# The last routed second products put between chunks of the first ones, and a fourth inner layer transposed by PE

## The chip, the cores and the metric

The kernel runs on one core of a Trainium2 chip. The metric is device time in microseconds (us) of one execution. Five executions of the kernel before took 523.51 to 530.28 us, with a median of 528.0 us. One further execution was profiled; its own time stands beside its span in the table below.

## The reference

The input x has 4 batches of 512 rows of width 512 (2,048 rows in all). A cross-attention is added first, then a feed-forward layer with one shared expert and eight routed ones, of which each row uses two:

```
x = x + tanh(g_xattn) * attention(layernorm(x), ctx)
z = layernorm(x)
swiglu(z, Wg, Wu, Wd) = (silu(z @ Wg) * (z @ Wu)) @ Wd      # D = 512, H = 352
top_v, top_i = top_k(sigmoid(z @ Wr + br + rb), 2); top_v normalised to sum 1
x = x + tanh(g_ffn) * (swiglu(z, shared) + sum over e of w[:, e] * swiglu(z, expert e))
```

All numbers are float32.

## The kernel before, in words

**Up to the routed experts** the kernel makes the attention of the four batches, the first product of the shared expert, the routing (which writes a list of rows for each expert), and the second product of the shared expert, whose result it writes to the output in device memory. The weights of all eight routed experts then stay in one buffer (`wbig`).

**The routed experts** take the list in blocks of 128 rows that belong to one expert. There are at most `NBLK` = 39 blocks; `SURE` = 37 of them are always made, numbers 0 to 36 (`last` = 36), and two more only if the routing needs them (`spare_blocks`, under a condition that was false here). The whole loop is written out when the program is built. A block i has these steps:

- `gather(i)`, L752: four indirect DMAs, issued from POOL, fetch the block's rows into one of four buffers. The gather of block i+3 is made to wait for the silu of block i.
- `block_turned(i)`, L822: DVE turns the rows (a stream transpose of 128x512, L326) into one of two buffers `xgT_v[i % 2]`. It can't be written before the first product of block i-2 has read it.
- `block_hidden(i)`, L779: the **first product**. `part(cs)` makes, for each chunk c of `ND` = 4, one matmul into `rg` and one into `ru` (L790, each of them two passes on PE in the profile). `finish()` then makes silu on ACT (L798) and the multiplication on DVE, into the inner layer `hr_v[i % 2]` (L800, or in two pieces at L810 for the blocks that PE transposes).
- The inner layer must be transposed before the second product can use it. For blocks below `SURE - NEAR` it goes through device memory: `hidden_moved(i)`, L825, issues two SP DMAs (L764 writes, L767 reads back into one of three buffers `zhr_v`), and DVE turns what came back (128x384, L326) into `hTr_v[i % 2]`. For the last `NEAR` = 3 blocks, 34, 35 and 36, `hidden_transposed_near(i)`, L837, has PE transpose it in three pieces (L840) and DVE copy the result out of PSUM (L841).
- `block_second(k)`, L843: the **second product** of three matmuls (L570, six passes in the profile), then ACT scales the result by the rows' weights (L817, into one of three buffers `y_v`) and POOL issues one indirect DMA (L818) that adds the 128 rows to the output in device memory. Each of these adds waits for the one before it, because all of them write the same output.

**The order.** Iteration i of the loop makes the first product of block i and then the second product of block i-2; that is the lag. Behind the loop stands block 36 with what is then left over:

```
    part, finish = block_hidden(last)
    hidden_transposed_near(last - 2)
    block_second(last - 2)
    part([0])
    hidden_transposed_near(last - 1)
    block_second(last - 1)
    part(range(1, ND))
    finish()
```

and after that the transposes and the second product of block 36 itself. Within an engine the instructions run in a fixed order. That order is not the order of the lines: when the program is built, a planner takes for each engine the earliest written instruction that its own model holds for ready. So the trace can have an instruction ahead of one that is written before it.

Of the kernel before, what the change touches and what calls it, by code (L numbers as in the profile page):

```python
# [22 lines left out]
def flamingo_block(  # L23
# [25 lines left out]
    NS, ND, NCC, NN = S // P, D // P, C // P, N // P  # L49
# [79 lines left out]
    zhr_v = [sp.take(NQ, HQ) for _ in range(3)]  # L129
    hTr_v = [sp.take(NF, P) for _ in range(2)]  # L130
    assert sp.at <= (B - 1) * NS * D

    def after(later, earlier, reason="written before it is read"):
        tc.add_manual_dep(
            later.ins, earlier.ins.name,
            mybir.DependencyInfo(mybir.DependencyClass.Sync, mybir.DependencyReason.DATA),
            reason=reason,
        )
# [185 lines left out]
    def turn(z, dst):  # L324

        return nc.vector.transpose(  # L326
            dst.rearrange("p c (j b) -> p b c j", b=NQ), z.rearrange("p b (c i) -> p b c i", i=Q)
        )
# [237 lines left out]
    def down(hT, wdj):  # L566

        po = ps_out.tile([P, D], F32, tag="out", name="po")
        for j in range(NF):
            product["last"] = nc.tensor.matmul(  # L570
                po, lhsT=hT[:, j, :], rhs=wdj(j), start=(j == 0), stop=(j == NF - 1)
            )
        return po
# [27 lines left out]
    def shared_out(b, lo=0, hi=NS, behind=None):  # L601
        for n in range(b * NS + lo, b * NS + hi):
            if n == 0:
                shared_turned(0, behind[0])
                shared_turned(1, behind[1])
            elif n + 1 < B * NS:
                shared_turned(n + 1)
            shared_back(n + AHEAD, product.get("out"))
            done = product["out"] = shared_down(n)
        return done  # L610
# [141 lines left out]
    def gather(i, behind=None, z=None):  # L752
        z = zx_v[i % 4] if z is None else z
        for q in range(NQ):
            g = nc.gpsimd.indirect_dma_start(  # L755
                out=z[:, q, :], out_offset=None,
                in_=xz_d, in_offset=at(idx4[:, q, i : i + 1]),
            )
            if behind is not None:
                after(g, behind, "not too many at once")  # L760
# [11 lines left out]
        nc.gpsimd.memset(h[:, H:], 0.0)  # L772

    n_used = nc.values_load(total_i[0:1, 0:1], min_val=0, max_val=NBLK)
    NEAR = 3
    SURE = NBLK - 2
    base = {}

    def block_hidden(i, xgT=None):  # L779
        xgT = xgT_v[i % 2] if xgT is None else xgT  # L780
        base[i] = nc.tensor.value_load(
            eoff_i[0:1, i : i + 1], min_val=0, max_val=(E - 1) * EW
        )
        pg = ps_mm.tile([P, H], F32, tag="mm", name="rg")
        pu = ps_mm.tile([P, H], F32, tag="mm", name="ru")

        def part(cs):
            for c in cs:
                for dst, lo in ((pg, 0), (pu, H)):
                    nc.tensor.matmul(  # L790
                        dst, lhsT=xgT[:, c, :],
                        rhs=wbig[:, bass.ds(base[i] + (c * 2 * H + lo), H)],
                        start=(c == 0), stop=(c == ND - 1),
                    )

        def finish():
            sg, h = sgr_v[i % 2], hr_v[i % 2]
            silu = nc.scalar.activation(sg, pg, AF.Silu)  # L798
            if i < SURE - NEAR:
                nc.vector.tensor_mul(h[:, :H], sg, pu)  # L800
                return silu

            full = H // HQ
            to = h.rearrange("p (c a i) -> p a c i", a=NQ, i=Q)
            for a, n, w in ((0, full, HQ), (full, 1, H - full * HQ)):
                x2, y2 = (
                    v[:, a * HQ : a * HQ + n * w].rearrange("p (a c i) -> p a c i", a=n, i=Q)
                    for v in (sg, pu)
                )
                nc.vector.tensor_mul(to[:, a : a + n, : w // Q, :], x2, y2)  # L810
            return silu

        return part, finish

    def block_out(i, po):
        y = y_v[i % 3]
        nc.scalar.activation(y, po, AF.Copy, scale=wts[:, i : i + 1])  # L817
        nc.gpsimd.indirect_dma_start(  # L818
            out=out, in_=y, out_offset=at(idx[:, i : i + 1]), in_offset=None, compute_op=ALU.add
        )  # L820

    def block_turned(i):  # L822
        return turn(zx_v[i % 4], xgT_v[i % 2])

    def hidden_moved(i):  # L825
        regroup(
            hr_v[i % 2], zhr_v[i % 3],
            dram.tile([NQ * P, HQ], F32, tag=f"by{HQ}", name="by", bufs=4),
        )
# [3 lines left out]
    turned = block_turned(0)  # L833
# [3 lines left out]
    def hidden_transposed_near(i):  # L837
        pt = ps_tr.tile([P, NF, P], F32, tag="tr", name="pt")
        for c in range(NF):
            nc.tensor.transpose(pt[:, c, :], hr_v[i % 2][:, ts(c, P)], ident)  # L840
        nc.vector.tensor_copy(hTr_v[i % 2], pt)  # L841

    def block_second(k):  # L843
        po = down(
            hTr_v[k % 2], lambda j: wbig[:, bass.ds(base[k] + (GU + j * D), D)]
        )
        block_out(k, po)

    def spare_blocks():

        sp = Space(wsd.rearrange("p c d -> p (c d)"), 0)
        zs = [sp.take(NQ, D // NQ) for _ in range(SURE, NBLK)]
        xgT = sp.take(ND, P)
        with tc.If(n_used > SURE):
            for i in range(SURE, NBLK):
                gather(i, z=zs[i - SURE])
            for i in range(SURE, NBLK):
                turn(zs[i - SURE], xgT)
                part, finish = block_hidden(i, xgT)
                part(range(ND))  # L860
                finish()
                hidden_transposed_near(i)
                block_second(i)


    last = SURE - 1
    for i in range(last):
        part, finish = block_hidden(i)
        part(range(ND))
        if i >= 2:  # L870
            turn(zhr_v[(i - 2) % 3], hTr_v[i % 2])
        nxt = block_turned(i + 1)
        if i == 0:
            after(nxt, turned, "its rows come later")
        silu = finish()
        if i < SURE - NEAR:
            hidden_moved(i)
        if i >= 2:
            block_second(i - 2)
        else:  # L880
            shared_out(B - 1, NS - 2 + i, NS - 1 + i)
        if i + 3 < SURE:
            gather(i + 3, silu)
        if i == last // 2:
            spare_blocks()

    part, finish = block_hidden(last)
    hidden_transposed_near(last - 2)
    block_second(last - 2)
    part([0])  # L890
    hidden_transposed_near(last - 1)
    block_second(last - 1)
    part(range(1, ND))
    finish()
    hidden_transposed_near(last)
    block_second(last)

# [53 lines left out]
```

## Time and profile before

| what | us |
|---|---|
| median of five executions | 528.0 |
| the profiled execution, its own time | 531.76 |
| its span, from the first to the last instruction | 529.8 |
| PE busy | 501.0 (95%) |
| POOL busy | 264.7 (50%) |
| DVE busy | 229.3 (43%) |
| ACT busy | 93.8 (18%) |
| PE busy from 260 to 480 us, of 220.00 | 219.18 |
| PE busy from 510 to 520 us, of 10.00 | 6.45 |

Starts are in us from the start of the span. "Matmul x2" in a row of the timeline is one float32 matmul of two passes. PE is the matmul engine, PEld its weight loads, SPq the DMA queue of SP. A bracket at the end of a row gives the engine's idle time before the instruction and what ended it.

### The profile page before, as it was taken

What the parts mean: (1) busy time and instruction counts of PE and PEld (TensorE: products, weight loads), DVE (VectorE), ACT (ScalarE), POOL (GpSimd) and SP (SyncE); (2) the same over time, 40 slices, a digit from 0 to 9 for tenths busy, and PEclk for the clock granted to TensorE, in tenths of its full rate; (3) what the DMA queues carried; (4) which work ended last, traced back from release to release, by engine and by line L of the source; (5) the groups of instructions that cost most, each with busy time, mean ns of one, the idle gap of its engine ahead of it and who ended that gap; (6) DMA issues with size and microseconds to landing.
All of it is one profiled execution on the core that took longest, in us unless ns stands there. A gap on an engine that the chain in (4) does not pass through costs nothing. (4 is left out here: it accounts for less than half of the span.)

```text
span 529.8 us, 5475 instructions
## 1 busy us (share of the span) xinstructions
PE 501.0 (95%) x1523; PEld 279.0 (53%) x1523; DVE 229.3 (43%) x542; ACT 93.8 (18%) x167; POOL 264.7 (50%) x290
## 2 busy tenths in 40 slices
PE   8999999998899959999999999999999999999981
PEld 4444564563577624445555555555555555555540
DVE  1898867842954206663423332233323332323210
ACT  3354035001042000000111111111111111111110
POOL 3005222170172620506677777777667777777231
PEclk9999999999799979999999999999999999999997
DMA  6999994398639998643466666666646566676333
GB/s 214 394 334 367 354 322 127 122 220 111 227 96 199 197 143 264 195 158 110 119 133 123 127 120 127 137 119 132 117 110 129 111 129 135 134 139 120 60 41 40
DMA packets 66590, 86.82 MB, mean 164 GB/s; under 512 B 32929, under 2 KB 39969, under 8 KB 66561
## 3 DMA queue, kind: packets, MB, share of 16 engines
q1 hardware_dynamic: 42480, 54.03, 35.0%
q0 software_dynamic: 13184, 25.88, 26.5%
q10 hardware_dynamic: 10896, 6.56, 5.2%
q8 instruction: 15, 0.25, 0.2%
q14 instruction: 15, 0.11, 0.1%
HBM read 55.73 MB, written 30.70 MB: 163 GB/s over the span
## 5 line engine op out<-in xcount | busy, mean ns | idle before, releaser
L755 POOL DMA_INDIRECT x_all<-xz_d,idx x148 | 141.3, 955 | 86.1 <-issue 35.7
L326 DVE STREAM_TRANSPOSE x_all<-x_all 128x512 f32<-128x512 f32 (+1 forms) x71 | 70.0, 986 | 159.5 <-DMA x_all<-by 131.1
L790 PE MATMUL rg<-wbig,x_all 128*128 x296 | 111.9, 460 | 1.7 <-issue 0.9
L790 PE MATMUL ru<-wbig,x_all 128*128 x296 | 111.7, 459 | 0.0
L570 PE MATMUL po<-wbig,x_all 128*128 x222 | 101.4, 592 | 0.7 <-DVE x_all L841 0.7
L790 PEld LDWEIGHTS rg<-wbig,x_all 128*128 128x128 f32 x296 | 55.9, 190 | 43.1 <-issue 18.4
L818 POOL DMA_INDIRECT out_x<-ws,idx x37 | 59.6, 1611 | 31.5 <-issue 17.5
L790 PEld LDWEIGHTS ru<-wbig,x_all 128*128 128x128 f32 x296 | 56.2, 190 | 31.3
L570 PEld LDWEIGHTS po<-wbig,x_all 128*128 128x128 f32 x222 | 42.1, 190 | 44.0 <-issue 36.3
L393 PE MATMUL po<-wbig 128*128 128x512 f32 x128 | 59.6, 618 | 3.4 <-DVE x_all L397 3.4
L466 PE MATMUL pg<-ws,wbig 128*128 128x352 f32 x128 | 50.6, 477 | 0.0
L466 PE MATMUL pu<-ws,wbig 128*128 128x360 f32 (+1 forms) x128 | 50.0, 473 | 0.0
L312 POOL TENSOR_TENSOR rstd<-ve,mhalf 128x4 f32<-128x4 f32 x8 | 8.2, 1022 | 79.3 <-DVE ve L310 39.2
L798 ACT ACTIVATE h_all<-rg 128x352 f32<-128x352 f32 x37 | 17.1, 463 | 171.9 <-PE rg L790 171.9
L570 PE MATMUL po<-wsd,wqk 128*128 128x512 f32 x96 | 42.3, 595 | 2.1 <-DVE eoff_i L700 2.1
L817 ACT ACTIVATE ws<-po,wts 128x512 f32<-128x512 f32 x37 | 25.4, 687 | 104.0 <-PE po L570 101.2
L393 PEld LDWEIGHTS po<-wbig 128*128 128x128 f32 x128 | 25.2, 199 | 34.8 <-issue 29.2
L554 POOL DMA_INDIRECT slot_d<-ent,posi x32 | 31.0, 967 | 24.2 <-DVE ent L543 10.5
L466 PEld LDWEIGHTS pu<-ws,wbig 128*128 128x128 f32 x128 | 24.9, 195 | 14.1 <-issue 1.0
L570 PEld LDWEIGHTS po<-wsd,wqk 128*128 128x128 f32 x96 | 18.0, 190 | 24.1 <-issue 20.3
L466 PEld LDWEIGHTS pg<-ws,wbig 128*128 128x128 f32 x128 | 23.8, 195 | 11.9 <-issue 1.0
L800 DVE TENSOR_TENSOR x_all<-h_all,ru 128x352 f32<-128x352 f32 x34 | 17.5, 516 | 12.5 <-PE ru L790 6.7
(133 smaller groups left out, 339.0 us busy)
## 6 DMA issues: line engine op xcount, KB each, us to landing
wbig<-in_Wgu SPq DMA_DIRECT2D x8, 1408.0 KB, 15.5
by<-x_all SPq DMA_DIRECT2D x34, 192.0 KB, 3.4
x_all<-by SPq DMA_DIRECT2D x34, 192.0 KB, 2.4
wbig<-in_Wd SPq DMA_DIRECT2D x8, 768.0 KB, 17.6
x_all<-in_x SPq DMA_DIRECT2D x4, 1024.0 KB, 11.9
wbig<-in_xT SPq DMA_DIRECT2D x4, 1024.0 KB, 10.0
xz_d<-wbig POOLq DMA_DIRECT2D x16, 256.0 KB, 4.7
out_x<-x_all SPq DMA_DIRECT2D x16, 256.0 KB, 3.0
```

The source lines that it names most:

```text
L312: power = nc.gpsimd.tensor_tensor(rstd, ve, mhalf, ALU.pow)
L326: return nc.vector.transpose(dst.rearrange("p c (j b) -> p b c j", b=NQ), z.rearrange("p b (c i) -> p b c i", i=Q))
L393: product["last"] = nc.tensor.matmul(po, lhsT=xT_v[b % 2][:, c, ts(s, P)], rhs=attT_v[b % 2][:, c, :], start=(c == 0), stop=(c == NN - 1),)
L466: product["last"] = nc.tensor.matmul(dst, lhsT=xnT_v[b % 2][:, c, ts(s, P)], rhs=ws[:, c, at : at + n], start=(c == 0), stop=(c == ND - 1),)
L554: sc = nc.gpsimd.indirect_dma_start(out=slot_d, in_=what, out_offset=bass.IndirectOffsetOnAxis(ap=where, axis=0), in_offset=None,)
L570: product["last"] = nc.tensor.matmul(po, lhsT=hT[:, j, :], rhs=wdj(j), start=(j == 0), stop=(j == NF - 1))
L755: g = nc.gpsimd.indirect_dma_start(out=z[:, q, :], out_offset=None, in_=xz_d, in_offset=at(idx4[:, q, i : i + 1]),)
L790: nc.tensor.matmul(dst, lhsT=xgT[:, c, :], rhs=wbig[:, bass.ds(base[i] + (c * 2 * H + lo), H)], start=(c == 0), stop=(c == ND - 1),)
L798: silu = nc.scalar.activation(sg, pg, AF.Silu)
L800: nc.vector.tensor_mul(h[:, :H], sg, pu)
L817: nc.scalar.activation(y, po, AF.Copy, scale=wts[:, i : i + 1])
L818: nc.gpsimd.indirect_dma_start(out=out, in_=y, out_offset=at(idx[:, i : i + 1]), in_offset=None, compute_op=ALU.add)
```

## The change

Four blocks instead of three have their inner layer transposed by PE: block 33 joins 34, 35 and 36 (`NEAR` = 4). The block behind the loop becomes a part of the loop. In the last four iterations the second products are written between the chunks of a first product, by a table whose keys are the iteration and the chunk ahead of which the product goes (`ND` = behind `finish()`) and whose values are the block: 31 ahead of chunk 3 of block 33; 32 ahead of chunk 2 of block 34; 33 ahead of chunk 1 of block 35 and 34 behind block 35; 35 ahead of chunk 3 of block 36. Block 36's own transposes and second product stay last.

```diff
-    NEAR = 3
+    NEAR = 4
...
     last = SURE - 1
-    for i in range(last):
+    seconds = {
+        (last - 3, 3): last - 5, (last - 2, 2): last - 4, (last - 1, 1): last - 3,
+        (last - 1, ND): last - 2, (last, ND - 1): last - 1,
+    }
+    for i in range(SURE):
         part, finish = block_hidden(i)
-        part(range(ND))
-        if i >= 2:
-            turn(zhr_v[(i - 2) % 3], hTr_v[i % 2])
-        nxt = block_turned(i + 1)
-        if i == 0:
-            after(nxt, turned, "its rows come later")
+        near = i > last - NEAR
+
+        def behind(c):
+            k = seconds[i, c]
+            if k < SURE - NEAR:
+                turn(zhr_v[k % 3], hTr_v[k % 2])
+            else:
+                hidden_transposed_near(k)
+            block_second(k)
+
+        if not near:
+            part(range(ND))
+            if i >= 2:
+                turn(zhr_v[(i - 2) % 3], hTr_v[i % 2])
+        else:
+            for c in range(ND):
+                part([c])
+                if (i, c + 1) in seconds and c + 1 < ND:
+                    behind(c + 1)
+        if i < last:
+            nxt = block_turned(i + 1)
+            if i == 0:
+                after(nxt, turned, "its rows come later")
         silu = finish()
         if i < SURE - NEAR:
             hidden_moved(i)
-        if i >= 2:
+        if near:
+            if (i, ND) in seconds:
+                behind(ND)
+        elif i >= 2:
             block_second(i - 2)
...
-    part, finish = block_hidden(last)
-    hidden_transposed_near(last - 2)
-    block_second(last - 2)
-    part([0])
-    hidden_transposed_near(last - 1)
-    block_second(last - 1)
-    part(range(1, ND))
-    finish()
     hidden_transposed_near(last)
     block_second(last)
```

## The prediction

> **What bounds the kernel now.** I first looked at the busy shares: PE is busy for 501.0 of 529.8 us, DVE for 43%, so I asked where PE waits in the stretch of the routed blocks, with the list of PE's waits from 260 us to the end and the busy times of two windows.
>
> ```profile
> PE 501.0 (95%) x1523; PEld 279.0 (53%) x1523; DVE 229.3 (43%) x542; ACT 93.8 (18%) x167; POOL 264.7 (50%) x290
> ...
> PE pt L840 <- DVE x_all L810: 0.8, 1, 0.8
> PE rg L790 <- ACTq L854: 0.8, 1, 0.8
> PE po L570 <- DVE x_all L841: 0.7, 1, 0.7
> ...
> 260.00:480.00 220.00, 219.18 (x660) 125.14 (x659) 69.88 (x91) 34.51 (x60) 162.96 (x151) 1.00 0.63 126
> 510.00:520.00 10.00, 6.45 (x19) 2.89 (x17) 1.14 (x3) 1.84 (x3) 2.18 (x2) 1.00 0.42 52
> ```
>
> The reader sees that from 260 us on PE waits three times, 0.8 us each; two of these lie in block 36: its transposes wait for the multiplication of its inner layer (L810), and its second product for the copy of the transposes (L841). Up to 480 us PE is full, at a granted clock of 1.00. Then the order of the last blocks, from the timeline. First PE and DVE around block 34's transposes:
>
> ```profile
> 502.41 0.49 PE L840 MATMUL pt<-ident,x_all 128*128 128x128 f32 x3
> 502.74 0.76 PE L790 MATMUL rg<-wbig,x_all 128*128 x2
> 502.94 0.56 DVE L841 COPY x_all<-pt 128x384 f32<-128x384 f32 x1 [2.26 <-PE pt L840]
> 503.33 0.75 PE L790 MATMUL ru<-wbig,x_all 128*128 x2
> 503.93 2.74 PE L570 MATMUL po<-wbig,x_all 128*128 x6
> ```
>
> The code has the second product directly behind the transposes and chunk 0 of block 36 after it. On the chip chunk 0 runs between the two, and the copy is hidden beneath it: the planner fills the gap. Then the adds to the output, from POOL's timeline:
>
> ```profile
> 490.62 1.61 POOL L818 DMA_INDIRECT out_x<-ws,idx  x1 [0.30 <-issue]
> 496.27 1.58 POOL L818 DMA_INDIRECT out_x<-ws,idx  x1 [4.04 <-ACT ws L817]
> 503.57 1.55 POOL L818 DMA_INDIRECT out_x<-ws,idx  x1 [5.72 <-ACT ws L817]
> 509.07 1.55 POOL L818 DMA_INDIRECT out_x<-ws,idx  x1 [3.94 <-DMA out_x<-ws,idx]
> 514.72 1.55 POOL L818 DMA_INDIRECT out_x<-ws,idx  x1 [4.09 <-issue]
> 520.22 1.57 POOL L818 DMA_INDIRECT out_x<-ws,idx  x1 [3.95 <-issue]
> ```
>
> These are the adds of blocks 31 to 36. Those of 32 and 33 waited for ACT, their own result. Those of 34, 35 and 36 waited for the add before them: they follow at 5.50, 5.65 and 5.50 us. The result of block 35 was ready at 511.53 (ACT 510.84 + 0.69), 3.2 us before its add went out; that of block 36 at 518.81, 1.4 us before. So **the end is set by the chain of adds, which begins with block 33's result**: 503.57 + 16.65 = 520.22, and 9.58 us from there to the end of the span. PE's last matmul alone would let the last add go at 518.81 + 0.27 = 519.08 (0.27 is what block 33's add took from its result, 503.30 to 503.57).
>
> **Prices, from rows of this trace.** A chunk (rg and ru) takes 1.18: the first product of block 33 runs from 480.49 to 485.22, a quarter of 4.73. A second product takes 2.58 (485.22 to 487.80). Three transposes take 0.33 of PE's stream (502.41 to 502.74). Without anything between, a second product starts 1.26 after its transposes (513.96 to 515.22), that is 0.93 of idle PE. Block 36's transposes start 1.00 after its last chunk (510.59 + 2 x 1.18 = 512.95, to 513.96): silu 0.46, multiplication 0.58, less the overlap with ru. From the start of a second product to its add, when nothing holds the add: 3.73 (499.84 to 503.57).
>
> **The change part by part.**
> *Block 33 by PE.* Removed: two SP DMAs (L764 at 486.02, L767 at 489.43) and one DVE turn of 0.87. Added: three transposes, 0.33 on PE, which is full and so pays it; a copy of 0.56 and 0.06 of multiplication (0.58 in two pieces against 0.52) on DVE, which has gaps of 4 to 5 us there. The DMAs removed were hidden: the turn of block 33 ended at 492.87 and its second product began at 499.84. So this part is +0.33 on PE, and +0.93 more if nothing covers the copy; the cover is a chunk of block 35, 1.18 long against 0.93.
>
> A row against a rule: the three transposes above take 0.33 us of the stream, 0.11 each. The Trainium skill, "TensorE: Matmul & The Clock Gate", Part 4 (PE-mode transpose), gives some 275 ns for one in a kernel and holds that transposes don't count as PE activity for the clock; by it block 33's three would be 0.83 and this part 0.5 dearer. The trace has the clock at 1.00 from 500 to 520 us with nine transposes in it, so I stay with the row.
>
> *The order.* I lay the same prices end to end from 480.49, where both kernels are still alike.
> Block 33: chunks 0 to 2 to 484.03, second product 31 to 486.61 (its turned input was there at 478.23), chunk 3 to 487.80. Block 34: two chunks to 490.16, second product 32 to 492.74 (its turn ended at 485.58), two chunks to 495.11. So far PE's work is the same as before, only in another order. Block 35: chunk 0 to 496.29, transposes 33 to 496.62, chunk 1 as filler to 497.80, second product 33 to 500.38, chunks 2 and 3 to 502.74, transposes 34 to 503.07, chunk 0 of block 36 as filler to 504.25, second product 34 to 506.83. Block 36: two chunks to 509.19, transposes 35 to 509.52, chunk 3 as filler to 510.70, second product 35 to 513.28. Silu and multiplication of block 36 now lie beside second product 35 (1.0 against 2.58), so the wait of 1.00 goes; transposes 36 start at 513.28, second product 36 at 513.28 + 1.26 = 514.54 instead of 515.22: 0.68 earlier (1.01 gained, 0.33 paid).
>
> *What is late next: the adds.* Results would let them go at 3.73 after each second product: 33 at 501.53, 34 at 507.98, 35 at 514.43; 36, by its own row, 3.86 after (515.22 to 519.08), at 518.40. The first three are further apart than the 5.5 that the chain needs. The last is not: it waits for the add of 35, 514.43 + 5.50 to 5.65 = 519.93 to 520.08. That is 0.29 to 0.14 before 520.22. So the second products come **more evenly, but the chain still ends the kernel, and it begins later**: with block 35 at 514.43 instead of block 33 at 503.57. Of PE's 0.68 some 0.2 is left. The sum: 529.8 - 0.2 = 529.6 for the span, 531.6 for the execution (1.96 lies outside the span), and 528.0 - 0.2 = 527.8 against the median; the profiled execution is 0.7% above the median, and since the edit is in the last 50 us I take the difference over as it is.
>
> A row against a rule for that cadence: the trace has 4.7 to 5.0 us from issue to landing of such an add of 256 KB. The Trainium skill, "DMA: Bandwidth & Descriptors", section "Anatomy of one DMA", has 2.0 us + bytes / 436e3, which I work out to an estimate of 2.6; by that the last add would not wait for the one before it, and the gain would be 1.8 instead of 0.2. The measured spacing decides.
>
> *Moved past queues.* Silu of block 33 comes 2.58 later, at 487.41 instead of 484.83. Behind it are the four gathers of block 36 on POOL: they then run from 488.15 to 492.9 (4 x 1.25), last rows in at about 495.8 (2.9 from the issue; the landing may take as little as 2.7). Block 36 starts on PE at 503.07, so PE has time. But add 31 is now ready at 487.8, before them; it must wait for add 30 (483.30 + 5.5 = 488.8), and if it stands ahead of them on POOL the rows come in at about 497 to 498. Behind them on DVE is the turn of block 36 (1.09), and possibly the copy of block 33.
>
> **Rivals.**
> *B, the fillers don't come* (slower). If the planner keeps the written order, three second products (33, 34, 35) wait 0.93 each, and block 36's 1.00 stays: second product 35 starts at 512.33, 36 at 518.36, its add at 522.2 (518.36 + 3.86), which is later than 516.06 + 5.5. That is +2.0 on the end: 530.0. It decides from the first of the gaps of 33 and 34 that stays open: 0.93 against the 0.2 gained. Against it: both gaps of the old order were filled, with a whole chunk each.
> *C, DVE stands behind the turn of block 36* (slower). If that turn is ahead of copy 33 in DVE's order and the gathers are late, the copy ends at about 499.7 to 500.0 instead of 497.2 and second product 33 starts 0.9 to 2.3 late. It decides when the rows come after 496.2. All later adds move by it: +0.7 to +2.1, so 528.7 to 530.1. For it: turns go out on DVE as soon as their buffer is free (493.29, straight behind block 34's multiplication); against it: the copy is written first.
> *D, the adds land faster* (faster). With two transfers fewer the spacing could fall below 4.0, and PE's end decides: add 36 at 518.4, -1.8: 526.2. Against it: the three spacings are alike, although the traffic beside them is not (DMA share 0.25 and 0.42).
> *E, the planner undoes it*, the products stay where they are and only the three transposes come in: +0.3, 528.3.
>
> **How the numbers follow.** A, the forecast, 0.56: 527.8. B 0.14, C 0.14, D 0.07, E 0.04; 0.05 for something that none of these rows shows. No case reaches 1% (5.3 us), which is about what a measurement of this kernel can tell from no change: the five runs lie 1.3% apart, the middle three 2.8 us. So faster by over 1% gets 0.03, within 1% 0.93, slower by over 1% 0.04. For the range I take 526.2 (D) to 530.1 (C) and add to each side about 1 us for the median of a few runs, less where the chance is small: 525.0 to 530.8.
>
> **What would show it.** Right: chunk 1 of block 35, chunk 0 and chunk 3 of block 36 between transposes and second products; no wait of PE for L810; one wait of 0.7 for L841 left; 33 turns of 128x384 in the routed stage instead of 34; the add of block 35 released by ACT, the last one by the add before it, at 5.5. Wrong: a wait of PE for L841 more than once (B), a DVE turn between block 34's multiplication and the first copy with PE idle behind it (C), a last add released by ACT (D), or a difference that arises before 480 us, which nothing here would explain.

## The result, and the profile after

| | before | changed |
|---|---|---|
| median of all runs | 528.84 us | 530.45 us |
| the profiled execution, its own time | 531.76 | 534.20 |
| its span | 529.8 | 531.8 |
| granted clock, mean over the span | 0.980 | 0.978 |

The ratio is 1.0037, with a 95% interval of 1.0019 to 1.0055: the changed kernel is slower by about 2.0 us (1.0 to 2.9), where 0.2 us faster was forecast. The ratio leaves out executions in a slower state that both kernels fall into at times, so it is not quite the ratio of the two medians.

The two executions are alike up to block 33: its first chunk starts at 480.49 before and at 480.38 after. From there to the end of the span it is 49.31 us before (529.8 - 480.49) and 51.42 after (531.8 - 480.38), **2.11 us more**. This stretch is used for all that follows, because it leaves out what other stages add to a single execution; from 480 to 520 us the granted clock is 1.00 in both.

The list of PE's waits from 260 us to the end of the changed kernel, with total, number and longest in us:

```profile
PE po L570 <- DVE x_all L841: 2.4, 3, 1.4
PE rg L790 <- ACTq L854: 0.8, 1, 0.8
```

The wait for the multiplication (L810) is gone, as forecast. But the second products wait three times for a copy of DVE instead of once, 2.4 us instead of 0.7. PE's timeline of the changed kernel, around the transposes of blocks 33 and 34 (start, length, instruction; the bracket is PE's idle time before it and what ended it):

```profile
496.18 0.49 PE L840 MATMUL pt<-ident,x_all 128*128 128x128 f32 x3
496.51 0.76 PE L790 MATMUL rg<-wbig,x_all 128*128 x2
497.11 0.76 PE L790 MATMUL ru<-wbig,x_all 128*128 x2
499.26 2.84 PE L570 MATMUL po<-wbig,x_all 128*128 x6 [1.40 <-DVE x_all L841]
...
504.30 0.49 PE L840 MATMUL pt<-ident,x_all 128*128 128x128 f32 x3
504.63 0.76 PE L790 MATMUL rg<-wbig,x_all 128*128 x2
505.68 2.84 PE L570 MATMUL po<-wbig,x_all 128*128 x6 [0.29 <-DVE x_all L841]
508.36 0.76 PE L790 MATMUL ru<-wbig,x_all 128*128 x2
```

Behind the transposes of block 33 the filler came, a whole chunk, and yet PE stood idle for another 1.40 us. At block 34 only the first matmul of the chunk (rg) stands in the gap; ru comes behind the second product. What held the copy of block 33 is in DVE's timeline of the same kernel:

```profile
495.26 0.58 DVE L810 TENSOR_TENSOR x_all<-h_all,ru 128x288 f32<-128x288 f32 x2 [5.71 <-ACT h_all L798]
497.74 1.08 DVE L326 STREAM_TRANSPOSE x_all<-x_all 128x512 f32<-128x512 f32 x1 [1.90 <-DMA x_all<-xz_d,idx]
498.67 0.53 DVE L841 COPY x_all<-pt 128x384 f32<-128x384 f32 x1
504.57 0.58 DVE L810 TENSOR_TENSOR x_all<-h_all,ru 128x288 f32<-128x288 f32 x2 [5.37 <-PE ru L790]
505.07 0.55 DVE L841 COPY x_all<-pt 128x384 f32<-128x384 f32 x1
```

The 128x512 turn is that of block 36. It waits 1.90 us for its rows, DVE keeps its order, and the copy of 33, whose input was ready at about 496.7, starts behind it at 498.67. In the second pair the copy of 34 stands behind the multiplication of 35. The rows are late for a reason that POOL's timeline shows. Before, the first and the last of the four gathers of block 36:

```profile
485.56 0.98 POOL L755 DMA_INDIRECT x_all<-xz_d,idx  x1 [0.64 <-ACT h_all L798]
...
489.37 0.94 POOL L755 DMA_INDIRECT x_all<-xz_d,idx  x1 [0.30 <-issue]
```

and in the changed kernel the same two, among the adds (L818) of blocks 31 to 36:

```profile
489.24 1.58 POOL L818 DMA_INDIRECT out_x<-ws,idx  x1 [3.93 <-issue]
491.13 1.01 POOL L755 DMA_INDIRECT x_all<-xz_d,idx  x1 [0.30 <-issue]
...
494.99 0.94 POOL L755 DMA_INDIRECT x_all<-xz_d,idx  x1 [0.31 <-issue]
496.24 1.63 POOL L818 DMA_INDIRECT out_x<-ws,idx  x1 [0.30 <-issue]
503.15 1.58 POOL L818 DMA_INDIRECT out_x<-ws,idx  x1 [5.28 <-ACT ws L817]
509.52 1.57 POOL L818 DMA_INDIRECT out_x<-ws,idx  x1 [4.79 <-ACT ws L817]
516.57 1.56 POOL L818 DMA_INDIRECT out_x<-ws,idx  x1 [5.48 <-ACT ws L817]
522.24 1.57 POOL L818 DMA_INDIRECT out_x<-ws,idx  x1 [4.11 <-issue]
```

Before, the gathers stood ahead of add 31 (490.62). Now add 31 stands ahead of them and has waited 3.93 us, which the profile puts down to no releaser; it goes out 5.55 behind add 30 (483.69), the spacing of an add that waits for the one before it; the gathers start 5.57 us later (491.13 against 485.56). The adds of 33, 34 and 35 each wait for their own result, as forecast, and the last waits for the one before it (5.67), as forecast; the whole row has moved back.

### The profile page after: what moved, and what is told of

Same layout as the page of the kernel before. It is cut to its first block, busy times and chain, and to the rows that moved or that the text cites. A ratio compares the mean times of both kernels' runs of the same rounds, so it can differ in the third digit from the quotient of the medians.

```text
span 531.8 us, 5475 instructions
## 1 busy us (share of the span) xinstructions
PE 502.0 (94%) x1526; PEld 279.2 (52%) x1526; DVE 230.1 (43%) x543; ACT 93.8 (18%) x167; POOL 265.0 (50%) x290
## 3 DMA queue, kind: packets, MB, share of 16 engines
q1 hardware_dynamic: 41808, 53.63, 34.3%
## 5 line engine op out<-in xcount | busy, mean ns | idle before, releaser
L818 POOL DMA_INDIRECT out_x<-ws,idx x37 | 59.7, 1613 | 33.8 <-issue 16.9
L570 PE MATMUL po<-wsd,wqk 128*128 128x512 f32 x96 | 43.9, 613 | 4.0 <-DVE eoff_i L700 4.0
```

The source lines that it names most:

```text
L570: product["last"] = nc.tensor.matmul(po, lhsT=hT[:, j, :], rhs=wdj(j), start=(j == 0), stop=(j == NF - 1))
L818: nc.gpsimd.indirect_dma_start(out=out, in_=y, out_offset=at(idx[:, i : i + 1]), in_offset=None, compute_op=ALU.add)
```

## The experiments

Three theories were put against each other, and the expectations name them so. **Theory 1**: the copy of 33 stands behind the turn of 36 on DVE, and that waits for late rows; without this order the loss is gone. **Theory 2**: the fourth block on PE and the new places of the second products cost it by themselves. **Theory 3**: POOL and the chain of adds set the end, whatever PE does. (In the last pair of runs "theory 3" is used once for something else: late rows that hold PE in any order of DVE.)

Three numbers of each trace are given below: the *lateness* of POOL, from the start of block 33's first chunk to add 30 (2.81 us where the four gathers of block 35, which stand ahead of it on POOL, go out as soon as the silu of block 32 is there); the *chain*, from add 30 to add 36; and the *stretch*, from the start of block 33 to the end of the span. The last add is always 9.4 to 9.8 us from the end, so the stretch is lateness + chain + about 9.6. Before: 2.81, 36.92, 49.31. After: 3.31, 38.55, 51.42.

### The turn of block 36 behind the copy of block 33

```diff
-        nc.vector.tensor_copy(hTr_v[i % 2], pt)
+        copied[i] = nc.vector.tensor_copy(hTr_v[i % 2], pt)
+
+    copied = {}
...
+            if i == last - 1:
+                after(nxt, copied[last - 3], "PE waits for the copy")
```

> The changed kernel with one dependency more: DVE's turn of block 36 comes behind its copy of block 33's transposes. That swaps these two on DVE and nothing else on any engine. Theory 1 (the copy stood behind a turn whose rows were late): second product 33 starts about 1.2 us after its transposes (about 497.7 us where blocks 33 begin at 480.4) instead of 3.1, no wait of PE above 0.5 us for L841 before block 36, and the last add moves from 522.24 to about 520.5, span about 530.1, 0.3 us above the kernel before (ratio about 1.000 to 1.001). Theory 2 (the fourth transposition on PE, or the new order of PE, costs the 2 us by itself): the last add stays at about 522, ratio about 1.004.

Measured: 524.75 us, ratio to before 1.0009 (0.9978 to 1.0040). The wait for the copy of 33 is gone. But in this execution POOL was late by 6.34, and the chain of adds ran at its own pace, 34.81, to a stretch of 50.62; the forecast place of the last add is missed for that reason. The same kernel again, later, on another chip:

> The changed kernel with the turn of block 36 behind copy 33, as in the first experiment, now beside the changed kernel on the same chip. Theory 1: the wait for copy 33 is gone wherever POOL stands (second product 33 at 1.5 us after its transposes), from the add of block 30 to the last one it is 34.8 us (38.6 to 40.4 in the changed kernel), and the ratio to the kernel before is 0.004 to 0.010 lower than that of the changed kernel: 1.000 to 1.001. Theory 2 (the fourth transposition or the new places cost it): the two ratios are alike.

Measured: 529.35 us, ratio 1.0052 (1.0007 to 1.0097). DVE's timeline of this run:

```profile
493.05 0.59 DVE L810 TENSOR_TENSOR x_all<-h_all,ru 128x288 f32<-128x288 f32 x2 [5.72 <-ACT h_all L798]
494.50 0.56 DVE L841 COPY x_all<-pt 128x384 f32<-128x384 f32 x1 [0.87 <-PE pt L840]
495.34 1.09 DVE L326 STREAM_TRANSPOSE x_all<-x_all 128x512 f32<-128x512 f32 x1 [0.28 <-DMA x_all<-xz_d,idx]
```

The copy waits for the transposes alone. With POOL late by 3.16, much as in the changed kernel, the chain is 36.97 and the stretch 49.63: 1.8 less than in the changed kernel and 0.3 more than before. In the traces this is theory 1. The times don't show it: the forecast was a ratio 0.004 to 0.010 below that of the changed kernel, which had 1.0029 (0.9986 to 1.0071) beside it, and 1.0052 is not below. With intervals of 0.3 to 0.45% to each side, such ratios can't tell theory 1 from theory 2.

### The rows early

The gathers of block 36 are released by the silu of block 32 instead of 33.

```diff
-        if i + 3 < SURE:
+        if i + 3 < last:
             gather(i + 3, silu)
+        if i + 4 == last:
+            gather(last, silu)
```

> The changed kernel with the gathers of block 36 released by the silu of block 32 instead of 33, so that they stand on POOL ahead of the add of block 30. The order on PE, DVE and ACT is that of the changed kernel: the turn of block 36 still stands ahead of copy 33. Theory 1: the rows are there when the turn's buffer is free (about 495.8), the copy ends at about 497.5, second product 33 starts at about 497.7, and the last add goes at about 520.5 to 520.7 (ratio 1.000 to 1.001), although the DVE order is the bad one. Theory 2: about 522, ratio about 1.004.

Measured: 527.10 us, ratio 1.0056 (1.0022 to 1.0089). The order on DVE is the bad one (turn 487.11, copy 488.05), and the second product of 33 starts 1.64 after its transposes with no wait on the copy: it is the lateness of the rows that makes the order cost something. Yet the forecast ratio of 1.000 to 1.001 was missed: the gathers now stand ahead of add 30, which goes out 10.05 after the start of block 33, and the adds follow 5.4 to 5.7 apart to a stretch of 53.29. Gathers and adds share POOL's queue; the chain of adds pays for what the rows gain.

### Three blocks on PE, in the new order

```diff
-    NEAR = 4
+    NEAR = 3
...
-        near = i > last - NEAR
+        near = i > last - 4
```

> The changed kernel's table with three blocks transposed by PE as before: block 33 goes through device memory again, so there is no copy 33 for the turn of block 36 to hold up. Theory 1: second product 33 starts straight behind chunk 0 of block 35 at about 496.2, second product 35 at about 510.9, the last add at 520.1 to 520.3, span about 529.8, ratio about 1.000. If the new places of the second products cost the 2 us themselves, the last add stays near 522 and the ratio at 1.004.

Measured: 525.25 us, ratio 1.0013 (0.9983 to 1.0043). Lateness 4.82, chain 34.89, stretch 49.28. With no copy of 33 on DVE there is nothing for the turn to hold, and the new places alone cost nothing that shows, although here too the adds are close behind one another and would hide a little.

### Four blocks on PE, in the old order

```diff
-    NEAR = 3
+    NEAR = 4
...
-        if i >= 2:
+        if i >= 2 and i - 2 < SURE - NEAR:
             turn(zhr_v[(i - 2) % 3], hTr_v[i % 2])
+        elif i >= 2:
+            hidden_transposed_near(i - 2)
```

> The kernel before with block 33 transposed by PE too, and nothing of the table. In the planned order the transposes of 33 and of 34 both stand ahead of second product 33, behind the whole of block 35, where no chunk covers the copy: second product 33 starts about 1.2 us later than before (about 501.0), and since the chain of adds begins with block 33 there, the last add moves from 520.2 to about 521.4: ratio about 1.002. If the chain of adds does not set the end, only the 0.33 us of the three transposes shows, ratio 1.000 to 1.001.

Measured: 525.95 us, ratio 1.0033 (0.9997 to 1.0069). Lateness 6.36, chain 34.81, stretch 50.93. The second product of 33 starts 1.24 behind the transposes, as forecast, but that is not what sets the end. This is the chain of the first run above within 0.01 us, although PE's order is the old one: where POOL is late, the adds set the end and hide what PE does. POOL's timeline of this run, the adds of 33 to 36:

```profile
497.32 1.55 POOL L818 DMA_INDIRECT out_x<-ws,idx  x1 [3.80 <-ACT ws L817]
502.94 1.55 POOL L818 DMA_INDIRECT out_x<-ws,idx  x1 [4.06 <-DMA out_x<-ws,idx]
508.49 1.55 POOL L818 DMA_INDIRECT out_x<-ws,idx  x1 [4.01 <-issue]
514.04 1.57 POOL L818 DMA_INDIRECT out_x<-ws,idx  x1 [3.99 <-issue]
```

They are 5.62, 5.55 and 5.55 apart. The profile names the add ahead as releaser only once; the even spacing, 1.9 to 3.6 us behind the results of 34, 35 and 36, speaks for the same in the other two.

### Both kernels again, unchanged

> The kernel before, unchanged, for a second profile beside those of the next three. In its first profile POOL came to the last blocks early: the add of block 30 went 2.8 us after block 33's first chunk, and the adds of 32 and 33 waited for their results. In the four experiments that went before, that add came 4.8 to 7.3 us after this chunk, and every add from there on waited for the one before it or for gathers: 34.8 us from the add of block 30 to that of block 36. Theory 3 (where POOL comes late, POOL's queue of gathers and adds alone sets the end, whatever the order on PE): if the add of block 30 comes over 5 us after the chunk here too, it is again 35 us from it to the last add, instead of 36.9.

The kernel before, unchanged: 531.27 us against 532.70 of the same program, ratio 0.9965 (0.9928 to 1.0002). So a ratio of 0.35% can come of nothing in a comparison of this size, and the times of single comparisons carry little here. In its trace POOL is late by 8.46, the chain is 35.54 (35 were forecast for such a lateness), the stretch 53.56. (The expectation's 4.8 to 7.3 and 34.8 for the four runs ahead of it are 4.8 to 10.1 and 33.5 to 34.9 in their traces.)

> The changed kernel, unchanged, beside the kernel before on the same chip. Theory 1: second product 33 starts about 3.1 us after its transposes here too, because the turn of block 36 stands ahead of the copy and its rows come late; the later POOL comes, the longer. Theory 3 adds: where POOL comes late in both kernels, both need 35 us from the add of block 30 to the last one, as the queue holds the same six adds and four gathers, and the stall of PE is partly hidden beneath it: ratio 1.000 to 1.003; where POOL comes early, 1.004 as measured so far.

The changed kernel, unchanged: 537.74 us, ratio 1.0099 (1.0063 to 1.0135). Lateness 6.05, chain 40.35, stretch 55.87. Theory 3 had 35 for this chain, too, and a ratio of at most 1.003: it fails here. The wait for the copy of 33 has grown with the lateness of POOL, since the rows come behind the adds:

```profile
495.44 0.49 PE L840 MATMUL pt<-ident,x_all 128*128 128x128 f32 x3
...
501.29 4.54 PE L570 MATMUL po<-wbig,x_all 128*128 x6 [4.18 <-DVE x_all L841]
505.67 0.76 PE L790 MATMUL rg<-wbig,x_all 128*128 x2
```

and the second product itself takes 4.38 (to 505.67) instead of 2.58; more of that below. A third profile of the changed kernel, beside the second run of the exchanged order:

> The changed kernel beside the next one on the same chip. Three profiles of this order gave a wait of PE for copy 33 of 1.40, 3.51 and 4.18 us where the add of block 30 went 3.31, 5.52 and 6.04 us after block 33's first chunk: the wait is this distance less 1.9. Theory 1: it is so again (within 0.2 us), and the ratio to the kernel before is 1.004 (early) to 1.010 (late).

Measured: 529.57 us, ratio 1.0029 (0.9986 to 1.0071). Lateness 2.82, wait 0.77, chain 38.16, stretch 50.64: 1.0 more than with the turn behind the copy. POOL was as early here as in the profile of before (2.81, 49.31), so like for like the change costs 1.33 in the traces; the rest of the 2.11 goes with a POOL that was 0.5 later.

### Without the add of block 35

This kernel leaves out the add of block 35 to the output.

```diff
+        if i == SURE - 2:
+            return
         nc.gpsimd.indirect_dma_start(
```

> The changed kernel without the add of block 35 to the output (the product and its scaling are still made). If the chain of adds sets the end, the last add goes as soon as its own result is there, 0.3 us after ACT's last scaling, or one spacing (5.5) after the add of block 34, whichever is later: 1.7 us earlier than in the changed kernel where POOL comes early (ratio to the kernel before about 1.000), 2.5 to 3 us earlier where it comes late (ratio about 0.995). If PE's end sets the end, nothing changes.

Measured: 536.41 us, ratio 1.0063 (1.0022 to 1.0103). Lateness 5.52, wait for the copy of 33 3.51, stretch 51.8. The last add goes out at 526.84, released by its own result; behind an add of 35 it would have been about 528.5 (result of 35 some 522.9, plus 5.6). So the last link of the chain is worth an estimated 1.7 us in this execution. The times don't show it: 0.995 was forecast where POOL comes late, and 1.0063 overlaps with the 1.0099 of the changed kernel beside it.

### Towards a version that beats both

Three blocks on PE in the new order, block 35's second product one chunk earlier, and the four gathers of block 36 put two and two around add 31, in an order given by dependences without a wait:

```diff
-        (last - 1, ND): last - 2, (last, ND - 1): last - 1,
+        (last - 1, ND): last - 2, (last, ND - 2): last - 1,
...
+            g = gather(last, early, qs=range(0, 2))
+            for one in g:
+                ordered(one, adds[last - 6])
...
+            if k == last - 5:
+                ordered(adds[k], g[-1])
+                rest.extend(gather(last, early, qs=range(2, NQ)))
```

> A version made to beat both: three blocks transposed by PE (block 33 through device memory), the second product of block 35 one chunk earlier than in the table, and the four gathers of block 36 split over two of the waits between adds (two behind the add of block 30, two behind that of block 31; they take 2.5 us each time, where POOL waits 3.9 for an add to land). Theory 3: from the add of block 30 to that of block 36 it is 33.6 us (six spacings of 5.6) instead of 35, so 1.0 to 1.4 us less than the kernel before, ratio 0.997 to 0.998. If POOL's queue does not set the end, the gain is at most the 1.0 us by which PE's end allows an earlier last add.

Measured: 532.68 us, ratio 1.0001 (0.9966 to 1.0036). POOL was late by 8.67, so the chain (34.26) set the end: stretch 52.54. The chain was forecast at 33.6; the forecast ratio, 0.997 to 0.998, lies inside the interval, but so does no gain.

A part of POOL's lateness lies in the code: in the kernel before, POOL falls some 3.4 us behind at the conditional blocks in the middle of the loop (the add of block 16 comes 1.93 after its result, that of block 17 5.37) and wins 0.34 a block back, all of it by block 28. In this run the adds are up to 4.3 behind their results ahead of that place already, and up to 7.8, at block 30, behind it; so its lateness doesn't come from there alone. The conditional blocks were put at the start of the loop, in the kernel before and in the one above:

```diff
-        if i == last // 2:
+        if i == 3:
             spare_blocks()
```

> The kernel before with the conditional part for the two spare blocks written behind block 3 instead of block 18; the condition is false, so nothing in it runs. In all profiles POOL falls 3.4 us behind at this part and regains 0.34 us with every block after it. Theory 3 (POOL's lateness in the last blocks is a part of the time): 15 blocks more to regain let the add of block 30 go up to 3.4 us earlier after block 33's first chunk where POOL comes late, and the ratio is 0.994 to 0.998 there; where POOL comes early anyway (2.8 us), nothing changes. If POOL's lateness does not matter, the ratio is 1.000.

Measured: 527.91 us, ratio 0.9983 (0.9942 to 1.0023). Lateness 2.81, stretch 49.45; POOL's lateness was 2.81 in the first profile of before as well, so this run had nothing to win and tells nothing of theory 3.

> The version with three blocks transposed by PE, the table with block 35 one chunk earlier and the gathers of block 36 split, with the spare part behind block 3 too: meant to beat both kernels. From the add of block 30 to the last one 33.6 to 34.3 us where POOL comes late, and POOL comes up to 3.4 us earlier: ratio 0.991 to 0.997; 0.998 where POOL comes early in the kernel before.

Measured: 527.91 us, ratio 0.9972 (0.9928 to 1.0016). Lateness 2.81, chain 36.33, the last five adds released by their own results, stretch 48.58: 0.73 less than before. That is the best stretch of all, and 0.14% of the time, which these runs can't tell from nothing.

### The same late rows in both orders

The cause stood in the traces, but the times were too close. So the rows were made later still: in both kernels the gathers of block 36 are ordered behind add 32, and the kernels differ in the order of two instructions of DVE. In the first the copy of 33 stays behind the turn of 36, as in the changed kernel; for that the turn is also written ahead of the copy:

```diff
+            if k == last - 3:
+                ordered(copied[k], nxt)
...
+        if i == last - 1:
+            nxt = block_turned(last)
...
-        if i < last:
+        if i < last - 1:
             nxt = block_turned(i + 1)
...
-        if i + 3 < SURE:
+        if i + 3 < last:
             gather(i + 3, silu)
+        if i + 2 == last:
+            gather(last, silus[last - 3], order=adds[last - 4])
```

> The gathers of block 36 are put behind add 32 on POOL (in the changed kernel they stand behind add 31), and the copy of block 33 stays behind the turn of block 36 on DVE, as in the changed kernel. Theory 1 (the copy of 33 is held by the turn of 36, and that by the rows): the rows land about 8.5 us after the add in front of the gathers; add 32 goes out about 16 us after the start of block 33 where POOL is not late, so the turn comes at about 23 to 25, second product 33 some 5 to 7 us later than in the changed kernel, less the chunk that PE can put in front. The last add moves by 4 to 5 us: from the start of block 33 to the end 55 to 58 us instead of 51, and the time is 1.0 to 1.6% over the kernel before. Theory 2 (the fourth transposition and the new places cost it, the rows do not): as the changed kernel, 51 us and +0.4%.

In the second it stands ahead of it:

```diff
+            if i == last - 1:
+                ordered(nxt, copied[last - 3])
```

> The same late gathers (behind add 32), but on DVE the turn of block 36 stands behind the copy of block 33. Theory 1: second product 33 starts some 1.5 us after its transposes with no wait on DVE's copy; the late rows can only hold the first chunk of block 36 and the multiplication of block 35, 0 to 2.5 us. From the start of block 33 to the end 50 to 52 us, time 0.1 to 0.5% over the kernel before, and at least 0.5% under the run with the copy behind the turn. Theory 2: no difference between the two runs. If late rows hold PE in any order (theory 3): both at 55 or more.

Measured: 536.53 us and ratio 1.0153 (1.0070 to 1.0236) for the first, 531.87 us and 1.0059 (1.0009 to 1.0108) for the second. POOL wasn't late in either (2.81 and 2.80). Stretch 57.67 and 50.34, the latter with the clock at 1.00 from 484 to 520 us: **7.3 us from the order of two instructions**, with what the planner made of it on PE, and with the lower clock behind the wait (last section). DVE's and PE's timeline of the first:

```profile
495.06 1.08 DVE L333 STREAM_TRANSPOSE x_all<-x_all 128x512 f32<-128x512 f32 x1 [6.87 <-DMA x_all<-xz_d,idx]
495.99 0.53 DVE L852 COPY x_all<-pt 128x384 f32<-128x384 f32 x1
496.58 5.13 PE L577 MATMUL po<-wbig,x_all 128*128 x6 [5.19 <-DVE x_all L852]
```

and of the second:

```profile
498.59 0.56 DVE L852 COPY x_all<-pt 128x384 f32<-128x384 f32 x1 [0.87 <-PE pt L851]
499.58 2.74 PE L577 MATMUL po<-wbig,x_all 128*128 x6
504.42 1.09 DVE L333 STREAM_TRANSPOSE x_all<-x_all 128x512 f32<-128x512 f32 x1 [5.27 <-DMA x_all<-xz_d,idx]
505.66 0.83 PE L799 MATMUL rg<-wbig,x_all 128*128 x2 [0.65 <-DVE x_all L333]
```

In the first, PE waits 5.19 for the copy, behind two chunks that the planner put into the gap. In the second, PE has no wait on the copy of 33, and the turn, late by about as much, holds PE's first chunk of block 36 for 0.65 only. The times differ by 0.94% in the same direction (some 5 us of 527); the ends of the two intervals still overlap, so it is the traces that settle it. Theory 2 expected the two alike.

## Why the prediction was wrong, point by point

**The step that failed is "Moved past queues".** It reckoned the gathers of block 36 straight behind the silu of 33, from 488.15 to 492.9, and the rows at 495.8. In the same paragraph it had seen that add 31 was ready at 487.8, ahead of them, and would have to wait for add 30 on the queue that both share; "if it stands ahead of them on POOL the rows come in at about 497 to 498". It did (489.24 after a wait of 3.93): the gathers ran from 491.13 to 495.93, the turn could start at 497.74, and the second product of 33 came 1.57 late, where the sum had nothing. The step's own 487.8, before 488.15, spoke for that order; its 488.8, the earliest for add 31 behind add 30, spoke against it. Which of them the planner goes by, no run shows. The step also counts the landing of 2.9 from the end of the last issue; it runs from its start (494.99 to 497.74 is 2.75), so by its own order its rows would have been there at about 494.8. What failed was that order on POOL.

**Rival C was the larger part of it**: +0.7 to +2.1 was its price, 2.11 us of stretch and 2.0 us of time were measured. That the whole meets C's upper end is luck: C's own part is 1.57 (0.9 to 2.3 in its terms), and a part of B, below, adds 0.57. The 499.7 to 500.0 that C gives for the end of the copy doesn't follow from its rows at 497 to 498 either (with 1.09 and 0.56 it is 498.7 to 499.7); 499.20 was measured. Its chance of 0.14 rested on "the copy is written first", against a reading of the trace that spoke for it (the turn stood straight behind a multiplication at 493.29 before, too). Its threshold was right: counted on the scale of the changed kernel, where block 33 starts at 480.38, the turn began at 497.74 in the changed kernel (wait 1.40), at 497.09 in its third profile (495.37, wait 0.77) and at 499.85 in the run without add 35 (504.07, wait 3.51). Each gives 496.3 as the time from which the rows cost PE; C had 496.2, which is 496.1 on this scale.

The terms, from the start of block 33 to block 35's second product, which starts at 512.83 where the sum, shifted by the 0.11 between the two executions, has 510.59:

- From the transposes of 33 to those of 34: 6.45 in the sum, 8.12 measured (496.18 to 504.30). 1.57 of the 1.67 is the late copy (second product at 499.26 instead of 497.69), 0.10 a second product that takes 2.68 behind a wait (499.26 to 501.94) instead of 2.58.
- From the transposes of 34 to those of 35: 6.45 in the sum, 7.02 measured. Here a part of **rival B** came true: the filler was rg alone; why the planner left ru for later stays open. PE idled 0.46 in the gap, of which the wait shows 0.29, and again 0.10. The wait is there with the turn behind the copy, too (0.29 in both of its runs), so it belongs to the new order and not to C.
- From the transposes of 35 to those of 36: 4.09 in the sum and 4.09 measured. The wait of PE for the multiplication of block 36 is gone.

1.67 + 0.57 = 2.24. The chain carries it on: add 35 goes out 3.74 behind its second product (forecast 3.73), the last one 5.67 later (forecast 5.50 to 5.65). Take C away and B's part stays: the exchanged order has a stretch 0.3 over before (49.63), where -0.2 + 0.57 would give 0.4.

**Right** were: PE's work is alike up to 480 us (POOL alone was 0.5 later by then); three transposes take 0.33 of PE; the removed DMAs were hidden; PE's first 15 us behind block 33's start are the same work in another order; the fillers at 33 and 35; the gain on PE at block 36; the last add held by the add before it, which is why D didn't come. PE's busy share of the last blocks, from the windows of the changed kernel (us, PE busy and its count, then PEld, DVE, ACT and POOL, the clock, DMA share and GB/s):

```profile
260.00:480.00 220.00, 219.18 (x661) 125.17 (x660) 68.92 (x90) 34.55 (x60) 162.59 (x151) 1.00 0.62 125
510.00:520.00 10.00, 8.71 (x28) 4.23 (x26) 1.70 (x4) 1.61 (x3) 2.65 (x2) 1.00 0.35 41
```

From 510 to 520 PE is busy for 8.71 of 10 us instead of 6.45. That is no sign of the evening out that was forecast: from 490 to 510 it is busy for 18.31 us instead of 20.00, and what it lost there it does later.

**Not foreseen** was how unsteady POOL is. The forecast took one execution, in which add 30 went out at its earliest (2.81). The traces here have it 2.8 to 8.7 after block 33's start (10.1 where the early gathers stand ahead of it). At 4.8 to 8.7 the chain of adds of before and of its variants without the held copy is 34.3 to 35.5, whatever PE's order, and none of the orders of second products tried there gains anything. The changed kernel loses more there, because its rows queue behind the same late adds: a wait of 0.77 at a lateness of 2.82, 1.40 at 3.31, 3.51 at 5.52, 4.18 at 6.05. Why POOL is late in some runs and not in others stays open. The conditional blocks make 3.4 us of it for a time, but in the kernel before all of that is won back by block 28, and to move them wasn't shown to pay.

## What to carry to other kernels

When a step is moved later, follow its DMAs onto the queue that issues them and ask which instruction is ready there first; then follow what waits for those DMAs onto its own engine, and ask what stands behind it in order. Here the turn of block 36, which PE read only 5.8 us after its end (498.82 to 504.63), kept the next copy from an engine that was idle. An order that a planner may choose should be pinned wherever an instruction that waits for a transfer can be put ahead of one that the bound engine is waiting for.

## What was unexpected of the hardware

A wait of PE can cost more than its length. Toward the end of the wait of 5.19 us the granted clock fell; the windows of that run (the kernel with later rows and the copy behind the turn; the clock is the third figure from the end):

```profile
490.00:492.00 2.00, 1.39 (x5) 0.57 (x3) 0.00 (x0) 0.00 (x0) 1.70 (x2) 1.00 0.62 132
492.00:494.00 2.00, 0.00 (x0) 0.00 (x0) 0.00 (x0) 0.00 (x0) 1.00 (x2) 1.00 0.12 33
494.00:496.00 2.00, 0.00 (x0) 0.00 (x0) 0.94 (x2) 0.00 (x0) 0.00 (x0) 0.60 0.13 33
496.00:498.00 2.00, 1.42 (x2) 0.84 (x3) 0.53 (x2) 0.00 (x0) 0.00 (x0) 0.50 0.00 0
498.00:500.00 2.00, 2.00 (x3) 0.68 (x2) 0.00 (x0) 0.00 (x0) 0.00 (x0) 0.50 0.00 0
500.00:502.00 2.00, 2.00 (x5) 0.98 (x4) 0.00 (x0) 0.21 (x1) 0.00 (x0) 0.70 0.00 0
```

The clock is 0.50 to 0.70 from 494 to 502 us, and the second product takes 4.96 (496.58 to 501.54) instead of 2.58: the wait costs 2.4 us on top of itself. Behind the wait of 4.18 the clock was 0.50 and 0.68 in the two windows from 502 to 506 us, and the second product took 1.8 us longer. Behind the wait of 3.51, in the run without add 35, it stayed 1.00:

```profile
507.00:509.00 2.00, 2.00 (x7) 1.07 (x6) 0.00 (x0) 0.48 (x1) 0.00 (x0) 1.00 0.01 1
```

The Trainium skill, "TensorE: Matmul & The Clock Gate", Part 1 (the HAM clock gate), has the clock fall to half after at least one idle window of some 3.4 us, and has the window run freely, not anew from a kernel's start. That agrees with all three: 4.18 and 5.19 fell, 3.51 didn't, which a free window allows, since an idle time little longer than it needs not hold a whole one. Where the windows lay in these runs, no trace shows. In the trace of before no wait from 260 us on was longer than 0.8, so it couldn't be seen there.
